# Cross attention with 20 heads: the second batch's output projection in 33 products over 512 tokens, and a written order for every step and transfer

## The chip, the cores and the metric

The kernel runs on one core of one Trainium2 chip. The core has a matrix engine (TensorE, PE in the profile), three engines for elementwise work (VectorE, DVE; ScalarE, ACT; GpSimd, POOL) and a queue that only starts transfers here (SyncE, SP). Data lies in SBUF, 128 partitions wide; TensorE reads SBUF and writes PSUM, eight banks of 128 x 512 numbers of 32 bits, and the other engines bring results back. The metric is the device time of one launch in microseconds (us), the median over several runs. The profile is one execution of the same program, recorded by the hardware; its span runs from the first to the last instruction.

## The reference

Two batches of 2048 tokens with 640 channels attend to 77 text tokens and, separately, to 77 further tokens ("ip"), each of 1024 channels, in 20 heads of 32 channels. All is 32-bit float.

```python
q = split_heads(x @ Wq.T)                       # 2 x 20 x 2048 x 32
k, v = split_heads(text @ Wk.T), split_heads(text @ Wv.T)
k_ip, v_ip = split_heads(ip @ Wk_ip.T), split_heads(ip @ Wv_ip.T)
out = attend(q, k, v) + attend(q, k_ip, v_ip)   # softmax(q k^T / sqrt(32)) v
return merge_heads(out) @ Wo.T + bo + x         # output projection and residual
```

The queries, the output projection and the residual work on 4096 rows of 640; keys and values have only 154 rows per batch.

## The kernel before, in words

All matrices come transposed: channels lie on partitions, in five chunks of 128, and tokens along the free side. A chunk of 128 channels holds four heads. The tokens of a batch are worked on in four blocks of 512 (`TB`), two blocks to a step of 1024 tokens. A step u from 0 to 19 is one chunk and one half of a batch: batch 0 has steps 0 to 9, batch 1 steps 10 to 19; q = u // 2 counts the pairs (chunk, batch) from 0 to 9.

**Names of the steps.** In step u, for three groups s of 384, 384 and 256 tokens: `Rs.u` computes scores on TensorE into four banks (L253), `Ks.u` takes them to SBUF on ScalarE (L265), `Ms.u` finds the row maxima on VectorE (L274), `Ss.u` subtracts them on GpSimd (L279), `Es.u` exponentiates on ScalarE (L285), `Ds.u` sums and inverts on VectorE (L292, L294), `Ns.u` multiplies on GpSimd (L299), and `Ts.u` transposes 32 x 32 blocks in place on VectorE (L306). `q.u.h` computes the queries of half h of step u (L221) and `cq` copies them out on ScalarE (L231). `A.q` multiplies the probabilities of both steps of a chunk with the values (L315) and `CA.q` copies the result to the tile `aT` on ScalarE (L338, L342). `k` and `v` project keys and values (L137), and `SQ` transposes the values in blocks (L148).

**Transfers.** SyncE's queue starts nearly all of them, one after another, in the order in which the program issues them. A block of x is 1280 KB (L207), five blocks' tiles do not fit, so the four tiles `xs` are loaded again and again: batch 1 reads each block once for each of its five chunks, from three of the tiles; the fourth, `xs[XROOM]`, holds sums of weights. The values of a chunk are spread over the tile `v4` in 16 small transfers of 20 KB (L175), two such tiles taking turns. A weight chunk for keys or values is 512 KB (`load_w`, L124), one for queries 320 KB (`load_wq`, L212). Before, these transfers are side effects of other steps: `load_next` issues an x block as soon as the queries that read its tile are issued, followed by the spreads still kept in the list `rest`, `begin` issues weights at the start of a step, and `attend` first issues the spreads left over.

**What sets the order.** `ORDERS` writes down, by hand and for each step, four queues of steps: PE, ACT, DVE and POOL. A loop (ahead of L917) emits from each queue the next step whose forerunners, listed in `need`, have been emitted. Each engine executes its own instructions in the order of emission and waits on semaphores where data of another engine is missing; the order across engines is set by data alone, and that of SyncE's transfers by the emission.

**Output projection.** For each block of 512 tokens the first four channel chunks in and out form a 512 x 512 weight matrix, which is multiplied in seven products of 2 x 2 blocks (a scheme of Strassen's kind) instead of eight. A product reads a sum of token rows (`sum_t`, GpSimd, L414) and a sum of weights (`sum_w`, GpSimd, L384), both of 256 columns per instruction on TensorE (L481); the fifth input chunk is added on top (L491). VectorE adds the banks to the residual tile (`take_product`, L506, L510, L512), which then goes out. The fifth output chunk is an ordinary product (`last_chunk`, L461, and `store_last`, L471). Batch 0's projection is interleaved with the steps of batch 1. For batch 1 all five chunks of attention are complete only after A.9 and CA.9, so its projection is the tail of the kernel:

```python
for m, i in ((1, 0), ("o", 0), ...):            # 28 products and 4 last chunks
    ...
    product(m, 1, i, at[(m, i)])                # 36 Matmults of 256 columns per block i
    take_product(m, 1, i, at[(m, i)])
```

Of the last chunks only the fifth input chunk is left for the tail (`p.0` to `p.3` do the rest before it). The residual of batch 1, all of its x, is loaded for the tail into `acc`, `res`, `pb` and slices of `xs` (L847, L851, L917).

Of the kernel before, what the change touches and what calls it, by code (L numbers as in the profile page):

```python
# [8 lines left out]
F32 = mybir.dt.float32  # L9
# [10 lines left out]
def kernel(  # L20
# [41 lines left out]
    SCALE = 1.0 / float(D) ** 0.5  # L62
    NP = B * NC
# [50 lines left out]
    loaded, used = [], set()  # L114

    def load_w(upto=len(wlist)):

        while len(loaded) < upto:
            n = len(loaded)
            if n >= len(wslots) and n - len(wslots) not in used:  # L120
                return
            src, c = wlist[n]
            w = wslots[n % len(wslots)]
            nc.sync.dma_start(  # L124
                out=w, in_=src[:, ts(c, P)].rearrange("(k p) o -> p k o", p=P)
            )
            loaded.append(w)
# [4 lines left out]
    def project_kv(n, out):  # L132

        load_w()
        t = n % 2
        for k in range(NCC):
            nc.tensor.matmul(  # L137
                keys_in(out), loaded[n][:, k, :], cT[:, k, :, t, :], start=(k == 0), stop=(k == NCC - 1)
            )
        used.add(n)  # L140
# [9 lines left out]
    rest = []  # L150

    def spread_v(q):


        spread_rest(len(rest))
        for g in range(G):
            for r in range(G):
                rest.append((q, g, r))
        spread_rest(G * G // 2 if q == NC - 1 else None)
        if q == NC - 1:  # L160
            rest.extend(["x", "wo"])

    def spread_rest(n=None):
        for _ in range(len(rest) if n is None else min(n, len(rest))):
            w = rest.pop(0)
            if w == "x" and n is None:
                return
            if w == "wo":
                nc.sync.dma_start(out=wo, in_=WoT.rearrange("(c p) o -> p c o", p=P))
                for part in PARTS:  # L170
                    fetch(0, part)
            if w in ("x", "wo"):
                continue
            q, g, r = w
            nc.sync.dma_start(  # L175
                out=v4s[q % 2][r * D : (r + 1) * D, g].rearrange("p k d -> p (k d)"),
                in_=squares(q)[g * D : (g + 1) * D],
            )
# [18 lines left out]
    def load_next(u, h):  # L197

        _, b, c, _ = step_of(u)
        n = place_of(u, h)  # L200
        if b == 0 and (c < NC - 1 or n == XROOM):
            return
        m = late.index((u, h)) + XROOM if b else n
        if m < len(late):
            v, g = late[m]
            tokens = ds(S + (step_of(v)[3] * NH + g) * TB, TB)
            nc.sync.dma_start(out=xs[n], in_=xT[:, tokens].rearrange("(k p) t -> p k t", p=P))  # L207
            spread_rest()
# [20 lines left out]
    def take_queries(u, h, pq):  # L229
        qT = qpool.tile([P, TB], F32, tag="qT", name=f"qT_{u}_{h}")  # L230
        nc.scalar.copy(qT, pq)  # L231
        qTs[(u, h)] = qT
# [38 lines left out]
    def maxima(u, s):  # L271
        n = GROUPS[s][1] * G
        mx = small.tile([P, n, 2], F32, tag=f"mx{n}", name=f"mx_{u}_{s}")
        nc.vector.tensor_reduce(mx, rows_of(u, s), AX.X, ALU.max)  # L274
        maxs[s] = mx

    def subtract(u, s):
        n = GROUPS[s][1] * G
        nc.gpsimd.tensor_tensor(  # L279
            rows_of(u, s), rows_of(u, s), maxs[s].unsqueeze(3).to_broadcast([P, n, 2, L]), ALU.subtract  # L280
        )

    def exponential(u, s):
        e = keys_of(u, s).rearrange("p n g l -> p (n g) l")
        nc.scalar.activation(e, e, AF.Exp, scale=SCALE)  # L285

    rdens = {}

    def sums(u, s):
# [5 lines left out]
        rdens[s] = rden  # L295

    def normalise(u, s):
        n = GROUPS[s][1] * G
        nc.gpsimd.tensor_tensor(  # L299
            rows_of(u, s), rows_of(u, s), rdens[s].unsqueeze(3).to_broadcast([P, n, 2, L]), ALU.mult  # L300
# [225 lines left out]
    for k in (0, half):  # L526
# [4 lines left out]
        load_w(k // half + 1)  # L531
    for _ in range(NH * NC):
        load_x()
    load_w()
# [11 lines left out]
    for t in range(2):  # L546
# [3 lines left out]
        for b in range(B):  # L550
            nc.scalar.copy(kT[:, 0, b, t, :], keys_in(ps)[:, b])

    ORDERS = {
        "0": (
            "1010", "430",
            "R0 R1 R2 F2 F0 F1",
            "K0 K1 K2 E0 E1 E2 C0 C2 C1",
            "M0 C0 M1 M2 D0 D1 D2 T0 C2 C1",
            "S0 S1 S2 N0 N1 N2",
        ),
        "1": (  # L570
            "1000", "26647",
            "F0 R0 R1 F3 F2 R2 F4 F1",
            "C0 K0 K1 K2 C2 E0 C3 C4 E1 E2 C1",
            "SQ M0 M1 T1- C3 C4 M2 T2- D0 D1 C0 D2 T0 C2 C1",
            "S0 S1 S2 N0 N1 N2",
        ),
        "even": (
            "1101", "310",
            "R2 R0 F2 R1 F0 F1 AT",
            "K2 K0 K1 E0 C0 C2 E1 C1 E2 CA",  # L580
            "C0 M0 T1- M1 T2- M2 D0 C2 C1 D1 D2 T0",
            "S0 S1 S2 N0 N1 N2",
        ),
        "odd": (
            "0010", "05244",
            "R0 F3 F0 R2 R1 F4 F2 F1",
            "K0 C3 C0 K2 K1 E0 C2 E2 C4 E1 C1",
            "M0 C4 C1 T1- M2 M1 SQ C2 D0 T2- D2 C0 C3 D1 T0",
            "S0 S2 S1 N0 N2 N1",
        ),  # L590
        "8": (
            "1100", "502",
            "R2 R0 F1 R1 F2 F0 AT",
            "K2 K0 K1 C2 C1 E0 C0 E2 E1 CA",
            "M2 C1 M0 T2- T1- M1 C0 D0 D2 D1 T0 C2",
            "S2 S0 S1 N0 N2 N1",
        ),
        "9": (
            "1101", "020",
            "R0 F0 R2 R1 F2 F1",  # L600
            "C0 K0 K2 K1 E0 E2 C1 C2 E1",
            "SQ M0 T2- C1 C2 M2 M1 D0 T1- C0 D2 D1 T0",
            "S0 S2 S1 N0 N2 N1",
        ),
        "10": (
            "1001", "4110",
# [12 lines left out]
        "12": (
            "0000", "7605",  # L620
            "R1 F0 F2 R0 F1 R2 F3 AT",
            "K1 K0 C0 C1 K2 E0 E1 CA E2",
            "C2 T2- M0 T1- M1 C3 M2 D0 D1 T0 D2",
            "S0 S1 S2 N0 G1 N1 N2",
        ),
        "13": (
            "0011", "560574",
            "F1 R0 F3 R1 R2 F2 F4 F5 F0",
            "K0 C1 K1 K2 E0 E1 E2 C0",
            "C3 M0 M1 M2 C2 T2- D0 D1 C5 D2 C4 T0 T1-",  # L630
# [24 lines left out]
            "0001", "46152",
            "R0 F2 R2 F1 R1 F3 F0 F4",
            "K0 K2 K1 C1 E0 E2 C0 E1",
            "M0 M2 C2 T1- T2- M1 C3 D0 D2 C4 D1 T0",
            "G2 S0 S2 G4 S1 N0 N2 N1",
        ),  # L660
        "18": (
            "0000", "5364",
            "R2 F2 R0 F1 R1 F0 F3 AT",
            "K2 K0 K1 E0 C0 E2 E1 CA",
            "C2 M2 M0 T1- M1 T2- D0 C3 D2 C1 D1 T0",
            "S2 S0 G1 S1 N0 N2 N1",
        ),
        "19": (
            "1110", "033657547",
            "R1 F0 F1 R0 F2 R2 F3 F7 F4 F6 F5 F8",  # L670
            "K1 K0 K2 E1 E0 E2",
            "C0 M1 T2- C1 M0 C2 M2 C3 T1- D0 C4 D1 D2 T0 C5",
            "G3 G2 S1 S0 G4 S2 N0 N1 N2",
        ),
        "20": (
            "0110", "6",
            "F0 AT",
            "CA",
            "T1- T2-",
            "",  # L680
        ),
    }

    OUTPUT = {
        10: "o0 20",
        11: "10 50 30 60",
        12: "70 40",
        13: "o1 21 51 11",  # L690
        14: "31 61",
# [7 lines left out]
    def kind_of(u):  # L699
        if str(u) in ORDERS:  # L700
            return str(u)
# [270 lines left out]
```

## Time and profile before

| what | value |
|---|---|
| time, median of 3 runs | 509.31 us (509.28 to 510.11) |
| span of the profiled execution | 506.7 us |
| granted TensorE clock | 1.000 |
| TensorE busy | 498.3 us, 98% |
| VectorE busy | 391.9 us, 77% |
| ScalarE busy | 242.5 us, 48% |
| GpSimd busy | 395.0 us, 78% |
| moved by transfers | 73.0 MB, mean 144 GB/s |

The page gives for each engine the time in which it executed something, and then the chain of work that ended last: followed back from the last instruction, at each step to what released it. A group of instructions is a line, an engine, an operation and its tiles, with its count, busy time, mean duration and the idle time just before. A 32-bit matmul leaves two records on PE and two weight loads. A table by stretches gives, for each stretch of the span, the length and then busy time and record count of PE, its weight loads, VectorE, ScalarE and GpSimd, then the granted clock, the share of the DMA engines and GB/s.

### The profile page before, as it was taken

What the parts mean: (1) busy time and instruction counts of PE and PEld (TensorE: products, weight loads), DVE (VectorE), ACT (ScalarE), POOL (GpSimd) and SP (SyncE); (2) the same over time, 40 slices, a digit from 0 to 9 for tenths busy, and PEclk for the clock granted to TensorE, in tenths of its full rate; (3) what the DMA queues carried; (4) which work ended last, traced back from release to release, by engine and by line L of the source; (5) the groups of instructions that cost most, each with busy time, mean ns of one, the idle gap of its engine ahead of it and who ended that gap; (6) DMA issues with size and microseconds to landing.
All of it is one profiled execution on the core that took longest, in us unless ns stands there. A gap on an engine that the chain in (4) does not pass through costs nothing.

```text
span 506.7 us, 10153 instructions
## 1 busy us (share of the span) xinstructions
PE 498.3 (98%) x4270; PEld 321.0 (63%) x4270; DVE 391.9 (77%) x347; ACT 242.5 (48%) x423; POOL 395.0 (78%) x163
## 2 busy tenths in 40 slices
PE   9999999999999999999999999999999999999997
PEld 5657557557656565456565656554755775588885
DVE  0079999999899987958997997699899999333333
ACT  1266666666676566645545636454654750100000
POOL 0079999989989988899999997798899999940000
PEclk9999999999999999999999999999999999999999
DMA  8982621331362453885574485168323242641213
GB/s 274 357 210 61 159 69 46 86 92 46 92 185 74 112 198 116 284 314 145 159 237 124 131 260 158 53 178 292 110 72 95 86 162 65 225 147 62 84 41 104
DMA packets 71053, 73.03 MB, mean 144 GB/s; under 512 B 5600, under 2 KB 50912, under 8 KB 71008
## 3 DMA queue, kind: packets, MB, share of 16 engines
q1 hardware_dynamic: 70288, 71.67, 45.9%
q8 instruction: 33, 0.54, 0.5%
q10 hardware_dynamic: 720, 0.72, 0.4%
q14 instruction: 12, 0.10, 0.1%
HBM read 58.61 MB, written 10.49 MB: 136 GB/s over the span
## 4 chain that ended last, share of the span: by engine, by line
PE 86%; DMA 5%; POOL 4%; DVE 1%; SPq 1%; issue 1%; ACT 0%; DVEq 0%; POOLq 0%
PE bank L221 31%; PE bank L481 18%; PE bank L253 9%; PE bank L315 9%; PE bank L137 9%; PE bank L461 5%; PE bank L491 5%; DMA x<-in_x_dram 3%; DMA wo_ct<-in_L_xattn_Wo_dram 2%; POOL pb L299 2%; POOL pb L279 1%; SPq L175 1%; POOL x L384 1%; DMA acc<-in_x_dram 1%; PE bank L541 1%
## 5 line engine op out<-in xcount | busy, mean ns | idle before, releaser
L279 POOL TENSOR_TENSOR pb<-pb,mx 128x1848 f32<-128x1848 f32 (+1 forms) x60 | 175.4, 2941 | 45.3 <-DVE mx L274 45.1
L221 PE MATMUL bank<-x,wq 128*128 128x512 f32 x400 | 180.7, 601 | 0.1
L299 POOL TENSOR_TENSOR pb<-pb,rden 128x1848 f32<-128x1848 f32 (+1 forms) x60 | 175.0, 2939 | 5.2 <-DVE rden L294 5.2
L274 DVE TENSOR_REDUCE mx<-pb 128x24 f32<-128x1848 f32 (+1 forms) x60 | 109.6, 1845 | 33.0 <-ACT pb L265 32.8
L265 ACT COPY pb<-bank 128x462 f32<-128x462 f32 (+1 forms) x240 | 101.7, 535 | 59.3 <-PE bank L253 58.5
L221 PEld LDWEIGHTS bank<-x,wq 128*128 128x128 f32 x400 | 74.1, 191 | 85.0 <-issue 81.7
L292 DVE TENSOR_REDUCE den<-pb 128x24 f32<-128x1848 f32 (+1 forms) x60 | 110.4, 1840 | 17.3 <-ACT pb L285 16.9
L285 ACT ACTIVATE pb<-pb 128x1848 f32<-128x1848 f32 (+1 forms) x60 | 94.9, 1582 | 56.4 <-POOL pb L279 56.2
L306 DVE STREAM_TRANSPOSE pb<-pb 128x1920 f32<-128x1920 f32 (+1 forms) x60 | 114.8, 1923 | 2.1 <-POOL pb L299 2.1
L253 PEld LDWEIGHTS bank<-kT,qT 32*128 32x128 f32 x1280 | 47.4, 184 | 26.3 <-issue 18.0
L253 PE MATMUL bank<-kT,qT 32*128 32x154 f32 x1280 | 58.7, 306 | 0.7 <-ACT vT L899 0.4
L315 PE MATMUL bank<-pb,v 32*32 32x512 f32 x1600 | 55.8, 597 | 1.2 <-ACT pb L265 0.7
L481 PE MATMUL bank<-aT,wo_ct 128*128 128x256 f32 x192 | 47.6, 382 | 1.0 <-DVE acc L512 0.7
L137 PEld LDWEIGHTS bank<-wo_ct,aT 128*128 128x128 f32 x320 | 43.1, 188 | 4.2 <-issue 3.5
L315 PEld LDWEIGHTS bank<-pb,v 32*32 32x32 f32 x1600 | 30.7, 103 | 23.2 <-issue 11.8
L137 PE MATMUL bank<-wo_ct,aT 128*128 128x154 f32 x320 | 45.3, 295 | 0.0
L481 PEld LDWEIGHTS bank<-aT,wo_ct 128*128 128x128 f32 x192 | 36.0, 190 | 11.0 <-issue 3.8
L231 ACT COPY qT<-bank 128x512 f32<-128x512 f32 x40 | 23.1, 588 | 31.4 <-PE bank L221 31.4
L461 PE MATMUL bank<-aT,wo_ct 128*128 128x512 f32 x80 | 36.1, 597 | 0.0
L506 DVE SCALAR_TENSOR_TENSOR pb<-bank,bo_sb,pb 128x256 f32<-128x256 f32 x24 | 10.5, 479 | 26.9 <-PE bank L491 16.4
L491 PE MATMUL bank<-aT,wo_ct 128*128 128x256 f32 x96 | 28.6, 379 | 0.0
L506 DVE SCALAR_TENSOR_TENSOR acc<-bank,bo_sb,acc 128x256 f32<-128x256 f32 x40 | 17.0, 466 | 13.3 <-PE bank L491 6.6
(47 smaller groups left out, 286.2 us busy)
## 6 DMA issues: line engine op xcount, KB each, us to landing
x<-in_x_dram SPq DMA_DIRECT2D x20, 1280.0 KB, 6.9
x<-in_x_dram SPq DMA_DIRECT2D x21, 256.0 KB, 5.2
out_dram<-acc SPq DMA_DIRECT2D x19, 256.0 KB, 2.8
acc<-in_x_dram SPq DMA_DIRECT2D x16, 256.0 KB, 6.7
v<-vS SPq DMA_DIRECT2D x160, 20.0 KB, 1.8
pb<-in_x_dram SPq DMA_DIRECT2D x3, 1024.0 KB, 7.6
wq<-in_L_xattn_Wq_dram SPq DMA_DIRECT2D x9, 320.0 KB, 4.8
aT<-in_L_xattn_Wk_dram SPq DMA_DIRECT2D x5, 512.0 KB, 5.6
```

The lines of the kernel that those rows point to most:

```text
L137: nc.tensor.matmul(keys_in(out), loaded[n][:, k, :], cT[:, k, :, t, :], start=(k == 0), stop=(k == NCC - 1))
L221: nc.tensor.matmul(pq, wqs[q % 3][:, k, :], xs[place_of(u, h)][:, k, :], start=(k == 0), stop=(k == NC - 1),)
L253: nc.tensor.matmul(ps[g][:, ts(t, 2 * L)], qTs[(u, h)][g * D : (g + 1) * D, ts(st, P)], kT[g * D : (g + 1) * D, c, b].rearrange("p t l -> ...
L265: nc.scalar.copy(keys_of(u, s)[:, :, g], ps[g][:, : n * 2 * L].rearrange("p (n l) -> p n l", n=n))
L274: nc.vector.tensor_reduce(mx, rows_of(u, s), AX.X, ALU.max)
L279: nc.gpsimd.tensor_tensor(rows_of(u, s), rows_of(u, s), maxs[s].unsqueeze(3).to_broadcast([P, n, 2, L]), ALU.subtract)
L285: nc.scalar.activation(e, e, AF.Exp, scale=SCALE)
L292: nc.vector.tensor_reduce(den, rows_of(u, s), AX.X, ALU.add)
L299: nc.gpsimd.tensor_tensor(rows_of(u, s), rows_of(u, s), rdens[s].unsqueeze(3).to_broadcast([P, n, 2, L]), ALU.mult)
L306: nc.vector.transpose(p, p)
L315: nc.tensor.matmul(pa[r][g * D : (g + 1) * D, :], v4s[q % 2][rows, g, k, :], zones[rows, :, g, k, :], start=(k == 0), stop=(k == NK - 1),)
L481: nc.tensor.matmul(part, w_of[m][:, kp, op], t_of(m, b, i)[:, kp], start=(op == kp == 0 and m in (1, 2, 5)), stop=(op == 1 and kp == 1 and ...
```

## The change

The hand-written queues and the loop that emitted from them are replaced by one list of words, `SCHEDULE`, emitted from first to last. A word names a step as above (with `@` and the bank or half of PSUM it writes); `G`, `W`, `m`, `cm`, `o`, `co` are batch 0's output projection. Transfers have words of their own: `LX.u.h` an x block, `VS.q.half` eight spreads, `LQ` and `LK` weights, `LO`, `LF`, `LW`, `LA` the output weights and residuals. The scale 1/sqrt(32) is applied where the queries are copied out, no longer in the exponential.

Batch 1's projection is written anew. It now treats its 640 x 512 weight part and the 2048 tokens as a whole: the inputs are split in five chunks of channels, the outputs in four, the tokens in two halves of 1024 columns. 33 products (`F`) take the place of 40: each is one weight block or sum of 128 x 128 (`weight`) times one token sum of 1024 columns (`tokens_of`), in two Matmults of 512 columns. 24 weight sums (`V`) run on VectorE, 25 token sums (`X`) on GpSimd (`.p`) or VectorE (`.d`). Eight chains (`CHAINS`) hold which products are accumulated in a bank in sequence and to which outputs the bank is added after each stage (`Y`, on VectorE); a later product of the chain accumulates on top of the same bank. `DIRECT` is empty, so `exponential_of` and the second form of `maxima` are not used. The sums go to tiles that are free by then: weight sums to the first part of `pb`, token sums to `xs[XROOM]`, to `aT`, to the rest of `pb`, and to rows of `aT` no longer read. The outputs are summed where the residual already lies: three x blocks stay in place after the last queries (`home`), and only the fourth is loaded (`LA`).

```diff
@@ transfers as steps of their own
-    def load_next(u, h):
...
-            nc.sync.dma_start(out=xs[n], in_=xT[:, tokens].rearrange("(k p) t -> p k t", p=P))
-            spread_rest()
+    def spread_v(q, half):
+
+        for g in range(G * half // 2, G * (half + 1) // 2):
+            for r in range(G):
+                nc.sync.dma_start(
+                    out=v4s[q % 2][r * D : (r + 1) * D, g].rearrange("p k d -> p (k d)"),
+                    in_=squares(q)[g * D : (g + 1) * D],
+                )
+
+    def load_block(u, h):
+
+        tokens = ds(S + (step_of(u)[3] * NH + h) * TB, TB)
+        nc.sync.dma_start(
+            out=xs[place_of(u, h)], in_=xT[:, tokens].rearrange("(k p) t -> p k t", p=P)
+        )
@@ the scale
-        nc.scalar.copy(qT, pq)
+        nc.scalar.mul(qT, pq, SCALE)
...
-        nc.scalar.activation(e, e, AF.Exp, scale=SCALE)
+        nc.scalar.activation(e, e, AF.Exp)
@@ the order
-    ORDERS = {
...
-    nc.sync.dma_start(out=last_of(1, XROOM), in_=in_dram_last(xT, 1, XROOM))
-    for i in range(1, NHB):
-        fetch_sums(i)
...
-        product(m, 1, i, at[(m, i)])
-        take_product(m, 1, i, at[(m, i)])
...
+    SCHEDULE = (
...
+        "N1.5 M0.6 R1.6@1 S0.6 T1.5 LQ.6 LK.17 v.3.0@3 LK.16 K1.6 VS.2.1 q.8.0@1 M1.6 E0.6 LQ.5 cv.3.0 T2.5 "
+        "cq.7.1 S1.6 M2.6 A.2@1 LX.10.0 D0.6 LK.15 S2.6 E1.6 cq.8.0 D1.6 N0.6 E2.6 D2.6 CA.2 R0.7@0 k.4.1@4 "
...
+        "VS.8.1 m6.1 G4.1 m2.2@5 E1.14 cm6.1 N0.14 LX.16.1 LX.17.0 cq.16.0 D1.14 LX.18.0 VS.7.0 R0.15@0 N2.14 "
...
+        "cm7.1 S2.15 E0.15 M1.15 D0.15 E2.15 m4.1 S1.15 LX.17.1 co.2 q.17.0@0 D2.15 N0.15 E1.15 cm4.1 cq.16.1 "
...
+        "R2.16@0 q.18.0@6 K2.16 T1.15 S0.16 M2.16 M1.16 E0.16 S2.16 A.7@0 LX.19.1 cq.17.1 D0.16 S1.16 E2.16 "
+        "D2.16 N0.16 CA.7 VS.9.1 m5.2@4 E1.16 N2.16 m1.2@7 LX.18.1 cm5.2 VS.8.0 T0.16 cq.18.0 R0.17@0 m3.2 "
...
+        "p.1@4 M2.19 cm6.3 T1.18 G4.3 E0.19 m7.3 S2.19 D0.19 p.0@5 LW E2.19 cm7.3 N0.19 D1.19 m4.3 D2.19 "
+        "N1.19 p.2@7 T0.19 cm4.3 N2.19 T1.19 LA p.3@6 X.I.p@0 T2.19 A.9@0 V.A X.D.d@1 V.P V.F V.G X.A.d@2 V.Q "
+        "V.E V.T V.C V.L V.H V.U CA.9 V.M V.V V.J F31.0@0 V.D V.N V.X F31.1@1 V.S F0.1@1 X.S.d@3 F0.0@0 "
+        "X.L.p@4 z.2 Y0.0.11 F7.0@3 z.0 V.O yz.2 X.U.p@5 F25.1@2 Y0.1.11 F25.0@7 yz.0 Y6.1.10 z.1 X.K.p@6 "
+        "Y6.0.10 F7.1@5 yz.1 F23.1@1 Y2.1.21 F23.0@0 Y2.1.31 X.Q.p@7 Y2.0.31 z.3 Y0.0.01 F13.1@5 Y0.1.01 "
+        "X.C.p@8 F10.0@4 F24.0@0 Y3.0.21 F20.0@7 V.R F1.1@1 V.I V.B Y2.0.21 X.O.p@9 F20.1@2 yz.3 Y6.0.11 "
+        "F24.1@1 Y6.1.11 F29.0@7 X.T.p@10 F29.1@2 F11.0@4 Y6.1.21 F1.0@0 X.X.p@11 Y6.0.21 Y0.1.00 F10.1@6 "
+        "Y3.0.20 F13.0@3 Y0.0.00 X.G.p@12 F6.1@1 Y3.1.21 F3.0@4 F11.1@6 X.B.d@13 F15.1@5 V.K V.W F30.1@2 "
+        "Y3.0.00 X.E.p@2 F30.0@7 Y3.1.20 Y6.1.20 F21.0@4 F3.1@6 X.M.p@4 Y3.0.01 F8.1@2 Y3.1.00 F4.1@4 Y6.0.20 "
+        "Y6.1.30 X.W.p@5 F21.1@6 F19.1@2 Y3.1.01 F8.0@7 Y2.1.11 X.J.p@3 Y6.1.31 F4.0@6 Y6.0.30 F6.0@0 Y1.0.00 "
+        "F26.1@2 Y1.1.00 X.V.p@7 F15.0@3 Y7.1.21 F19.0@7 F26.0@5 X.N.p@6 Y6.0.31 F2.1@2 Y7.0.21 F22.0@7 "
+        "Y7.1.11 X.P.p@r41 F2.0@5 Y2.0.11 F5.1@2 Y7.0.11 F22.1@3 Y7.1.31 X.H.p@r21 F5.0@5 Y5.1.01 F27.1@2 "
+        "Y5.0.01 Y5.0.31 F18.1@1 X.R.p@r31 Y7.1.30 F16.0@7 Y0.1.10 F18.0@0 Y5.1.31 Y7.0.31 F9.0@7 X.Y.p@9 "
+        "Y0.0.10 F9.1@3 Y7.1.10 F27.0@5 X.F.d@13 F14.0@2 F14.1@0 Y4.0.31 F17.0@6 Y4.1.31 F16.1@3 Y7.0.10 "
+        "Y7.0.30 F12.0@2 Y5.1.21 F17.1@4 Y5.0.21 F12.1@0 Y4.0.00 Y1.1.20 F32.0@2 Y4.1.00 F28.0@2 Y1.1.30 "
+        "Y1.0.30 F32.1@0 Y1.0.20 F28.1@0 Y4.0.20 Y4.1.20 "
+    ).split()
...
+    R_SUMS = (
+        "+01-21 +30+11 +21-31 +31+11 +10-00 +11-10 +30-31 +30+10 +01-00 +01-11 +01-D +21-I +30+C +G+J +D-I "
+        "+M-20 +20-L +E+N +40-41 +11-41 +11-40 +10-40 +C-40 +C-41 +V+20 "
+    ).split()
+    W_SUMS = (
+        "+01+30 -32-13 +10+02 +34-24 +03-01 +01+20 +30+31 +20-E +D-22 +03-A +13-I -32-02+12 +00-10-20 "
+        "-12-10-13 +00+01+02 +14-04-34 -P-11 +H+22+23 +32-J+33 +Q-22-24 -G-01+21-22 +U+03-23 +13-V-33 "
+        "+01-Q-03-21+22+23 "
+    ).split()
+    PRODUCTS = (
+        "04 41, 02 Q, K C, M 00, 30 E, B M, L 20, 34 S, W 30, D X, "
+        "H K, F O, A R, N 21, J N, P T, R D, G F, 11 V, S G, "
+        "Q U, O I, E J, C L, 04 S, T 40, I W, 32 P, U H, X 11, "
+        "V B, 10 A, 22 Y"
+    ).split(", ")
+    CHAINS = (
+        "0,31:+11 23:+01 1,24:+00 6,18:+10",
+        "4:-00 17:-20-30",
+        "7:-21-31 13,15:-11",
+        "10:+21 11:+20 3:+00 21:+01",
+        "14:-31 12:+00 28,32:+20",
+        "22:+01+31 9,16:+21",
+        "25:-10 20:-11 29:-21 30:-20 8:-30 19:-31",
+        "26:-21 2:-11 5:-31 27:-10-30",
+    )
...
+    def place_for(text):
+        if text[0] == "r":
+            return tokens_of(text[1:])
+        n = int(text)
+        if n < 2:
+            flat = xs[XROOM].rearrange("p k t -> p (k t)")[:, ts(n, NH * TB)]
+        elif n < 4:
+            return aT[:, ds(NC * NHB + 2 * (n - 2), NH)]
+        else:
+            flat = pb_flat[:, ds(zone + (n - 4) * NH * TB, NH * TB)]
+        return flat.rearrange("p (i t) -> p i t", t=TB)
+
+    def tokens_of(w):
+        if w.isdigit():
+            return rows_of_attention(1, int(w[0]))[:, ds(NH * int(w[1]), NH)]
+        return places[w]
...
+    def add_part(o, ps, op):
+        t = sum_at(o)
+        if o in untouched:
+            untouched.discard(o)
+            nc.vector.scalar_tensor_tensor(t, t, bo_sb[:, o[0] : o[0] + 1], ps, ALU.add, op)
+        else:
+            nc.vector.tensor_tensor(t, t, ps, op)
+        parts_left[o] -= 1
+        if not parts_left[o]:
+            m, i = o
+            nc.sync.dma_start(out=outT[ts(m, P), ds(S + i * TB, TB)], in_=t)
+    def finish(k, args, where):
+        if k == "LW":
+            for kp in range(2):
+                nc.sync.dma_start(
+                    out=a21[:, kp],
+                    in_=WoT[ts(2 * kp, P), : (NC - 1) * P].rearrange("p (op s o) -> p s op o", s=2, o=P)[:, 1],
+                )
+        elif k == "LA":
+            for u, h in late[-XROOM:]:
+                home[step_of(u)[3] * NH + h] = xs[place_of(u, h)]
+            (fourth,) = set(range(NHB)) - set(home)
+            nc.sync.dma_start(
+                out=acc,
+                in_=xT[: (NC - 1) * P, ds(S + fourth * TB, TB)].rearrange("(o p) t -> p o t", p=P),
+            )
+            nc.sync.dma_start(out=res, in_=xT[ts(NC - 1, P), ds(S + fourth * TB, TB)])
+        elif k == "V":
+            out = weight(args[0])
+            (op, a), *more = terms(W_SUMS[number(args[0])])
+            if not more:
+                nc.vector.tensor_scalar(out, weight(a), -1.0, None, ALU.mult)
+            for n, (o2, b) in enumerate(more):
+                if n == 0 and op == ALU.subtract:
+                    nc.vector.scalar_tensor_tensor(out, weight(a), -1.0, weight(b), ALU.mult, o2)
+                else:
+                    nc.vector.tensor_tensor(out, weight(a) if n == 0 else out, weight(b), o2)
+        elif k == "X":
+            w, e = args
+            (_, a), (op, b) = terms(R_SUMS[number(w)])
+            ra, rb = tokens_of(a), tokens_of(b)
+            places[w] = place_for(where)
+            (nc.vector if e == "d" else nc.gpsimd).tensor_tensor(places[w], ra, rb, op)
+        elif k == "z":
+            i = int(args[0])
+            last_chunk(at[f"p.{i}"], 1, i, (NC - 1,))
+        elif k == "yz":
+            i = int(args[0])
+            add_part((NC - 1, i), at[f"p.{i}"], ALU.add)
+        elif k[0] == "F":
+            m, h = int(k[1:]), int(args[0])
+            c, s = stage_of[m]
+            first = (c, h) not in at
+            if first:
+                at[(c, h)] = banks[int(where)]
+            w, x = PRODUCTS[m].split()
+            nc.tensor.matmul(
+                at[(c, h)], weight(w), tokens_of(x)[:, h], start=first, stop=True, skip_group_check=True
+            )
+        elif k[0] == "Y":
+            c, h, t = int(k[1:]), int(args[0]), args[1]
+            add_part((int(t[0]), NH * int(t[1]) + h), at[(c, h)], sign_of[(c, t)])
+        else:
+            raise ValueError(k)
...
+    for word in SCHEDULE:
+        emit(word)
```

## The prediction

> **What bounds the kernel now.** I read the page's totals first, then its chain, then the table by stretches for the end, then groups, the chain and the DMA queue in order of time.
>
> ```profile
> span 506.7 us, 10153 instructions
> PE 498.3 (98%) x4270; PEld 321.0 (63%) x4270; DVE 391.9 (77%) x347; ACT 242.5 (48%) x423; POOL 395.0 (78%) x163
> ...
> PE 86%; DMA 5%; POOL 4%; DVE 1%; SPq 1%; issue 1%; ACT 0%; DVEq 0%; POOLq 0%
> ```
>
> TensorE works 98% of the span, at granted clock 1.00 in every stretch. So only fewer or shorter matmuls, or new gaps on PE, can move the end. Now the end, us of busy time by engine:
>
> ```profile
> 425.00:437.00 12.00, 11.78 (x175) 5.30 (x173) 5.60 (x5) 0.58 (x3) 11.92 (x9) 1.00 0.42 132
> 437.00:460.00 23.00, 22.89 (x98) 18.67 (x99) 9.36 (x17) 1.72 (x7) 11.70 (x10) 1.00 0.46 160
> 460.00:480.00 20.00, 20.00 (x95) 17.60 (x94) 7.13 (x14) 0.00 (x0) 0.00 (x0) 1.00 0.24 79
> 480.00:507.00 27.00, 22.98 (x107) 19.89 (x105) 8.69 (x17) 0.00 (x0) 0.00 (x0) 1.00 0.23 78
> ```
>
> From 437 PE (first figure after the comma) is full, DVE (third) works 25 us of 66, POOL (fifth) is done by 449. The chain there:
>
> ```profile
> 431.33 5.07 PE bank L315 x137
> 436.39 0.02 issue
> 436.42 0.66 ACT aT L342 x2
> ...
> 437.12 1.99 PE bank L481 x8
> 439.11 3.43 PE bank L461 x8
> ...
> 461.54 7.77 PE bank L481 x36
> ...
> 503.01 0.48 DVE pb L506
> ```
>
> A Matmult leaves two records. 36 records of 256 columns take 7.77 us, so such a Matmult costs 0.432 us; 8 of 512 columns take 3.43, so 0.858. The tail runs from 437.12 to about 503.0 (65.9 us), then 3.7 us to the span's end.
>
> **The change, part by part.** The words after A.9 are the tail; ahead of it the steps on PE, ScalarE, VectorE and GpSimd stand in the same order in both kernels. Only SP's order differs.
>
> *Products.* Gone: 4 blocks x 36 Matmults of 256 columns, 144 x 0.432 = 62.2 us. New: 33 products x 2 halves of 512 columns, 66 x 0.858 = 56.6. The four `z` steps stay, 3.4. PE's tail goes from 65.6 to 60.0: **-5.6 us**.
>
> *Weight sums.* 24 `V` words are 40 VectorE instructions of 128 columns, from SBUF to SBUF, which this trace does not have. Nearest rows:
>
> ```profile
> L512 DVE TENSOR_TENSOR pb<-pb,bank 128x512 f32<-128x512 f32 x9 | 6.2, 687 | 11.2 <-PE bank L481 5.7 <-PE bank L491 5.5
> L506 DVE SCALAR_TENSOR_TENSOR pb<-bank,bo_sb,pb 128x256 f32<-128x256 f32 x24 | 10.5, 479 | 26.9 <-PE bank L491 16.4 <-ACT aT L342 8.6 <-PE bank L481 1.9
> L148 DVE STREAM_TRANSPOSE vS<-vT 128x160 f32<-128x160 f32 x10 | 2.8, 315 | 1.2 <-ACT vT L899 1.2
> L414 POOL TENSOR_TENSOR x<-aT 128x512 f32<-128x512 f32 x10 | 12.6, 1269 | 0.0
> L384 POOL TENSOR_TENSOR x<-wo_ct 128x256 f32<-128x256 f32 x1 | 0.7, 742 | 0.0
> ```
>
> 687 and 479 ns for 512 and 256 columns extrapolate to 0.375 us; the 160-column transpose, busy 2.8/10, gives 0.28. I take 0.29, the row nearest in size. The last transpose ends at 430.6 (427.04 + 3.56). From there 31 of the 40 stand ahead of `X.S`, with the sums `X.D` and `X.A` (1024 columns; the 1280-column transposes take 1.48, so 1.2 each): 31 x 0.29 + 3 x 1.2 = 12.6, so S is ready at 443.2. PE, from 437.12, has F31, F31, F0, F0, z (5 x 0.858) until 441.4; F7 needs S. **+1.8 us** of gap; at 0.375 it is 4.5, and at 0.2 (below any row) none.
>
> *Outputs.* 62 `Y` and 4 `yz` at 0.69 are 45.5 us. With 11.6 for all V and 6.0 for five X.d, VectorE has 63 us between 430.6 and PE's end near 499: it fits, but idle drops from two thirds to a twelfth. `Y` also frees PSUM: a chain's next stage waits for it, and PE is then late. I add 0, bound 2.
>
> *GpSimd.* 256 and 512 columns (742, 1269) extrapolate to 2.33 us for 1024; 20 sums are 47 us. The first runs before A.9 ends; the others start at 436.7 and have until 499. Each of the early ones is ready 4 us or more ahead of its product (L at 439.0 for F23 near 448). Cost 0.
>
> *The port.* What a two-operand VectorE sum costs while GpSimd sums, no row shows: VectorE's sums now have one operand in PSUM, and beside them GpSimd's 1848-column sums keep 3284 ns. Bounds: nothing, or full exclusion (priced as a rival). I take nothing, the rows' own case, and keep the other end. The Trainium skill (SBUF — State Buffer, Who interferes with whom) speaks against it: two SBUF inputs on VectorE contend with a GpSimd instruction that reads SBUF, the later one waiting out the earlier. By it 18 sums alternate with GpSimd's from 436.7 and the result is the second rival's; by the rows it is the sum below.
>
> *Transfers.* Residual loads shrink, as three x blocks stay in place; `LW` (two of 256 KB; such loads land in 3.6 us) goes out after the store at 420.5 and lands near 425, ahead of 430.6. Both are hidden by 5 us or more. The order costs more. Each transfer waits for the eighth before it, and small ones land behind big ones:
>
> ```profile
> 198.24 6.54 DMA x<-in_x_dram
> 204.79 0.51 SPq L175
> ```
>
> An x block lands in 6.3 to 6.5 us, 16 spreads take 16 x 0.63 = 10.1 us of issue. (a) `LX.18.1` now stands behind VS.9.1, whose eight issues start when A.7 (350.8) lets v4 go, about 355.5, so it is issued at 360.4 and lands at 366.7; q.18.1 starts at 365.29 in this trace: **+1.3**. (b) VS.2.1 stands behind LQ.6, LK.17 and LK.16, 1.3 MB issued at 136 that take some 8 us (54.78 to 63.17 in this trace): its last spread lands near 144.5, A.2 is due at 143.55: **+0.9** (0 to 1.6). (c) VS.7.0 stands behind three x blocks, so LX.17.1 goes out at 334 and lands at 340.5 to 342; q.17.1 is due at 341.1, 340.2 without (d): **+0.9** (0 to 2.5). (d) The gap at 331 disappears: there an x block and 16 spreads hold the acc load back to 320.9 and PE waits 0.66 for DVE: **-0.9** with its drain. Sum **+2.2**, bounds -0.9 to +4.5. Gaps near 180 to 191 (3 us) come from ScalarE and stay.
>
> *ScalarE's* scale moves from 60 exponentials to 40 query copies of unchanged shape. 0.
>
> Sum: -5.6 + 1.8 + 2.2 = **-1.6**: span 505.1. The median of the runs shown (509.31) is 2.6 above the profiled span; with that kept, 507.7.
>
> **Rivals.** *VectorE keeps the port while its sums run back to back; GpSimd starts after S.* For it: its queue has no wait among them. Then 19 sums start at 443.2, and V.O, R, I, B, K, W and two X wait up to 2.33 us, which VectorE's spare time half covers: +1 to +4, so 510.
>
> *The engines alternate, one sum each* (the other side). At 436.7 VectorE has done A, D, P, F, G, A and 8 more: 18 of 31 remain. GpSimd has ten sums ready (L to E); the eleventh overwrites L and needs F23, behind F7. So S comes 10 x 2.33 = 23 us later, PE stands idle with it, and the later V and X add 0 to 6: 507.7 + 23 + 0..6, say 533. It decides as soon as three sums wait in turn. Against it: no such wait has a row.
>
> *VectorE becomes the bound.* If V costs 0.375 and Y 0.75 (the 512-column row with bias), its 63 us become 71 from 430.6: last add at 502, no gain, and the transfers' 2.2 remain: 512.
>
> *The change does not do what it says*: 132 records for 288, as the order shows; no chance.
>
> **How the numbers follow.** No contention 0.45 (507.7; own range 504.5 to 511), VectorE first 0.20 (510; 507 to 513), alternation 0.25 (533; 527 to 538), VectorE bound 0.10 (512). 0.2%, 1.0 us, is about what a measurement tells from no change. Faster: 0.6 of the first, 0.35 of the second: 0.35. Same: 0.2, 0.3 and little: 0.16. Slower: 0.49. The range must take half of the alternation: 504.5 leaves out 0.05 below, 533 some 0.13 above.
>
> **What would show it.** Right: L481/L491 gone after A.9, 132 records 0.429 apart, one PE gap of 1 to 3 us four products in, 128-column VectorE sums near 0.29 at any time, GpSimd's near 2.33 from A.9's end; x blocks ending PE's waits before q.17.1 and q.18.1. Wrong: a long VectorE stretch between V.L and X.S with 2.3 us per sum (alternation), GpSimd's second sum starting after X.S (VectorE first), PE gaps ended by DVE all along (VectorE the bound).

## The result and the profile after

| | before | changed |
|---|---|---|
| time, median of 4 runs each | 509.68 us (509.28 to 510.11) | 545.6 us (542.57 to 549.3) |
| ratio, 95% interval | 1 | 1.0715 (1.0666 to 1.0765) |
| span of the profiled execution | 506.7 us | 545.2 us |
| granted clock, mean over the span | 1.000 | 0.969 |
| A.9 starts at | 431.3 us | 444.9 us |
| from there to the span's end | 75.4 us | 100.3 us |

The change makes the kernel 7% slower. The last two rows split the 38.5 us by which the two profiled executions differ (the medians differ by 35.9): 13.6 are lost before the new tail begins, 24.9 in it. The page of the changed kernel (totals, then its chain):

```profile
span 545.2 us, 9882 instructions
PE 503.0 (92%) x4114; PEld 295.7 (54%) x4114; DVE 453.5 (83%) x410; ACT 242.5 (44%) x423; POOL 423.2 (78%) x167
...
PE 74%; DVE 15%; DMA 6%; ACT 2%; issue 1%; SPq 1%; POOL 1%; DVEq 0%
```

TensorE has 156 records fewer and is busy longer, since part of its work ran at a lower clock; it is now idle for 42 us of the span. VectorE, 1% of the chain before, has 15% of it. The same four stretches of the end as in the prediction (busy time of PE, its weight loads, VectorE, ScalarE, GpSimd; then clock, DMA share, GB/s):

```profile
425.00:437.00 12.00, 12.00 (x40) 7.58 (x41) 11.61 (x12) 5.98 (x7) 10.40 (x6) 1.00 0.33 101
437.00:460.00 23.00, 17.96 (x191) 8.25 (x190) 22.72 (x30) 2.31 (x8) 16.86 (x8) 1.00 0.21 69
460.00:480.00 20.00, 3.43 (x4) 1.52 (x5) 18.78 (x17) 0.00 (x0) 14.05 (x6) 0.51 0.03 13
480.00:507.00 27.00, 23.03 (x53) 9.84 (x51) 22.96 (x29) 0.00 (x0) 17.40 (x8) 0.98 0.08 30
```

From 460 to 480 PE does 3.4 us of work at clock 0.51, while VectorE is busy for 18.8 us with 17 instructions, 13 of them sums of 128 columns that take 1.2 us each on average. The timeline of VectorE there (start, duration, instruction); A.9 ends at 450.4:

```profile
443.89 0.71 DVE L812 TENSOR_TENSOR pb<-wo_ct 128x128 f32<-128x128 f32 x1
...
450.44 0.28 DVE L812 TENSOR_TENSOR pb<-wo_ct 128x128 f32<-128x128 f32 x1
450.75 7.03 DVE L812 TENSOR_TENSOR pb<-pb,wo_ct 128x128 f32<-128x128 f32 x3
457.71 2.42 DVE L812 TENSOR_TENSOR pb<-wo_ct,pb 128x128 f32<-128x128 f32 x1
460.05 2.42 DVE L812 TENSOR_TENSOR pb<-wo_ct 128x128 f32<-128x128 f32 x1
462.40 2.42 DVE L810 SCALAR_TENSOR_TENSOR pb<-wo_ct 128x128 f32<-128x128 f32 x1
...
475.30 1.22 DVE L818 TENSOR_TENSOR aT<-aT 128x1024 f32<-128x1024 f32 x1
```

and of GpSimd:

```profile
442.09 2.35 POOL L818 TENSOR_TENSOR x<-aT 128x1024 f32<-128x1024 f32 x1
450.58 2.35 POOL L818 TENSOR_TENSOR pb<-aT,x 128x1024 f32<-128x1024 f32 x1 [6.14 <-DVE pb L812]
452.89 2.39 POOL L818 TENSOR_TENSOR pb<-aT 128x1024 f32<-128x1024 f32 x1
455.25 2.38 POOL L818 TENSOR_TENSOR pb<-aT,x 128x1024 f32<-128x1024 f32 x1
457.60 2.38 POOL L818 TENSOR_TENSOR pb<-aT,pb 128x1024 f32<-128x1024 f32 x1
...
471.67 2.38 POOL L818 TENSOR_TENSOR aT<-aT 128x1024 f32<-128x1024 f32 x1
485.94 2.35 POOL L818 TENSOR_TENSOR pb<-aT,pb 128x1024 f32<-128x1024 f32 x1 [11.89 <-PE bank L832]
```

GpSimd sums follow each other every 2.35 us, and each VectorE sum ends just after a GpSimd sum ends: 457.71 + 2.42 = 460.13, the GpSimd sum begun at 457.60 ended at 459.98. It is one for one. Before 450.58 such VectorE sums took 0.28, all but the first: it met the GpSimd sum begun at 442.09 and lasted 0.71, until just after that one's end at 444.44. The tiles of these two have nothing in common, so it is no dependence in the program that makes the one wait for the other. After ten sums GpSimd stops (its next one overwrites L, which a later product still reads), VectorE's last sums run freely, and the row at 475.30 is X.S, the sum for which F7 waits. The waits of PE from 450 on (what it waited for: us in total, times, longest):

```profile
PE bank L832 <- DVE aT L818: 21.3, 1, 21.3
PE bank L832 <- DVE acc L779: 4.7, 1, 4.7
PE bank L832 <- ACT aT L338: 0.3, 1, 0.3
```

The second is the later cluster (X.B, K, W, at 498 to 507). VectorE's adds out of PSUM are untouched by GpSimd: the groups of the tail in one table show 36 of them at 683 ns (such adds took 687 in the kernel before), with one operand in PSUM, and 20 weight sums, both operands in SBUF, at 1004.

```profile
L779 DVE TENSOR_TENSOR x<-x,bank 128x512 f32<-128x512 f32 x36 | 23.6, 683 | 8.2 <-PE bank L832 7.9
L812 DVE TENSOR_TENSOR pb<-pb,wo_ct 128x128 f32<-128x128 f32 x20 | 19.9, 1004 | 0.6
```

Of the 13.6 us ahead of the tail 0.7 stand at A.2 already, without an account here; the rest lies at three places. The table compares the start of each A with the kernel before:

| | A.2 | A.3 | A.6 | A.7 | A.8 | A.9 |
|---|---|---|---|---|---|---|
| later by, us | 0.7 | 3.0 | 2.9 | 7.1 | 13.6 | 13.6 |

Two of them are waits of PE for an x block, here in PE's timeline (q.17.1 and q.18.1; 10 records otherwise take 4.5, and the granted clock over these two is 0.73 and 0.59):

```profile
346.50 6.23 PE L191 MATMUL bank<-x,wq 128*128 128x512 f32 x10 [3.42 <-DMA x<-in_x_dram]
375.91 7.55 PE L191 MATMUL bank<-x,wq 128*128 128x512 f32 x10 [3.47 <-DMA x<-in_x_dram]
```

And the transfer queue ahead of both (start of the first issue, time to the end of the last one, count):

```profile
322.41 1.63 SPq L176 DMA_DIRECT2D x<-in_x_dram  x3
324.08 13.27 SPq L148 DMA_DIRECT2D v<-vS  x8
...
338.60 0.44 SPq L176 DMA_DIRECT2D x<-in_x_dram  x1
...
362.81 6.18 SPq L148 DMA_DIRECT2D v<-vS  x8
369.04 0.58 SPq L176 DMA_DIRECT2D x<-in_x_dram  x1
```

VS.7.0, eight small spreads behind three x blocks, takes 13.3 us to issue, since the eighth of them goes out at 336.8 only, when the third block has landed; LX.17.1 leaves at 338.6. LX.18.1 leaves at 369.0, behind VS.9.1, which had to wait for A.7.

### The profile page after: what moved, and what is told of

It reads as the page before. It is cut to its first block, busy times and chain, and to the rows that moved or that the text cites. A ratio compares the mean times of both kernels' runs of the same rounds, so it can differ in the third digit from the quotient of the medians.

```text
span 545.2 us, 9882 instructions
## 1 busy us (share of the span) xinstructions
PE 503.0 (92%) x4114; PEld 295.7 (54%) x4114; DVE 453.5 (83%) x410; ACT 242.5 (44%) x423; POOL 423.2 (78%) x167
## 4 chain that ended last, share of the span: by engine, by line
PE 74%; DVE 15%; DMA 6%; ACT 2%; issue 1%; SPq 1%; POOL 1%; DVEq 0%
PE bank L191 29%; PE bank L311 9%; PE bank L832 9%; PE bank L223 9%; PE bank L132 8%; DVE pb L812 6%; PE bank L477 6%; PE bank L457 3%; DMA x<-in_x_dram 3%; DVE den L288 2%; DVE mx L261 2%; DVE pb L302 2%; PE bank L487 2%; DMA aT<-in_L_xattn_Wk_ip_dram 1%; DMA wq<-in_L_xattn_Wq_dram 1%
## 5 line engine op out<-in xcount | busy, mean ns | idle before, releaser
L191 PE MATMUL bank<-x,wq 128*128 128x512 f32 x400 | 185.3, 614 | 7.4 <-DMA x<-in_x_dram 7.2
L191 PEld LDWEIGHTS bank<-x,wq 128*128 128x128 f32 x400 | 75.7, 195 | 95.5 <-issue 82.8
L311 PEld LDWEIGHTS bank<-pb,v 32*32 32x32 f32 x1600 | 31.8, 103 | 21.8 <-issue 10.1
L201 ACT ACTIVATE qT<-bank 128x512 f32<-128x512 f32 x40 | 23.7, 600 | 36.2 <-PE bank L191 36.2
L457 PE MATMUL bank<-aT,wo_ct 128*128 128x512 f32 x80 | 37.4, 609 | 0.0
L832 PE MATMUL bank<-aT,wo_ct 128*128 128x512 f32 x24 | 12.9, 642 | 21.6 <-DVE aT L818 21.3
L477 PE MATMUL bank<-aT,wo_ct 128*128 128x256 f32 x128 | 32.0, 382 | 0.0
L779 DVE TENSOR_TENSOR x<-x,bank 128x512 f32<-128x512 f32 x36 | 23.6, 683 | 8.2 <-PE bank L832 7.9
L477 PEld LDWEIGHTS bank<-aT,wo_ct 128*128 128x128 f32 x128 | 24.0, 190 | 6.7 <-issue 4.0
L457 PEld LDWEIGHTS bank<-aT,wo_ct 128*128 128x128 f32 x80 | 15.2, 193 | 17.8 <-issue 17.5
```

Source lines behind the costliest of these rows:

```text
L191: nc.tensor.matmul(pq, wqs[q % 3][:, k, :], xs[place_of(u, h)][:, k, :], start=(k == 0), stop=(k == NC - 1),)
L311: nc.tensor.matmul(pa[r][g * D : (g + 1) * D, :], v4s[q % 2][rows, g, k, :], zones[rows, :, g, k, :], start=(k == 0), stop=(k == NK - 1),)
L477: nc.tensor.matmul(part, w_of[m][:, kp, op], t_of(m, b, i)[:, kp], start=(op == kp == 0 and m in (1, 2, 5)), stop=(op == 1 and kp == 1 and ...
```

## The experiments

Theory: a VectorE sum of two SBUF operands waits out a GpSimd sum that is running, and the tail loses by that alone; the transfers' order loses the rest, each wait counting twice because the clock falls in it. Rivals: the sums are slow of themselves; the scale, the list or the new tail's loads make the start late; queries after a wait are slow for want of data.

**GpSimd held until X.S.** One small GpSimd instruction that reads X.S stands ahead of X.L:

```diff
             places[w] = place_for(where)
+            if w == "L":
+                s = places["S"][:, 0, :HT]
+                nc.gpsimd.tensor_tensor(places[w][:, 0, :HT], s, s, ALU.add)
```

> The changed kernel, with one GpSimd instruction of 256 columns put ahead of X.L that reads X.S, so that GpSimd's second to twentieth sums cannot start before VectorE has made S; its result is overwritten by X.L and nothing is left out. Theory A (a two-operand VectorE sum from SBUF waits out a GpSimd sum that is running, and the two alternate): the sums between A.9's end and X.S fall from 2.3 us each to 0.2 to 0.3, S is ready about 5 to 6 us after A.9's end instead of 26, PE's wait for it falls from 21.3 us to 0 to 2, and the recovery of its clock goes with it. GpSimd then starts 19 sums of 2.37 us some 5 us later, and later VectorE sums among them still wait: span 522 to 532 against 545.2. Theory B (the sums are long for a reason of VectorE's own, their operands or their place, and GpSimd only happens to run): they stay above 2 us with GpSimd idle, S comes as late as before, GpSimd starts 20 us later and the span goes to 555 to 565.

Span 532.7, A.9 at 444.1, tail 88.6. The sums ahead of X.S run at 0.2 to 0.3 us each, X.S begins 4.1 us after A.9's end (453.66 against 449.6) and PE waits 0.4 us for it in place of 21.3. The rival falls. The span missed the forecast by 0.7 because waits came up further on, here the waits of PE and two rows of VectorE's timeline in this kernel:

```profile
PE bank L833 <- DVE x L777: 6.1, 1, 6.1
PE bank L833 <- DVE acc L777: 5.1, 1, 5.1
PE bank L833 <- DVE x L775: 1.2, 1, 1.2
```
```profile
466.84 5.48 DVE L810 TENSOR_TENSOR pb<-pb,wo_ct 128x128 f32<-128x128 f32 x3
472.24 2.42 DVE L808 SCALAR_TENSOR_TENSOR pb<-wo_ct 128x128 f32<-128x128 f32 x1
```

These are V.R, V.I and V.B, which stand among the outputs and now meet GpSimd's sums; in the changed kernel GpSimd was pausing there. VectorE's queue is in order, so each holds the outputs behind it back, PSUM is not freed, and PE waits.

**The transfers of the kernel before, the new tail.** The words up to A.9 are put in the order in which the old loop emitted steps and transfers; each engine's own steps keep their order (of the diff, the last transfers alone):

```diff
-VS.8.1 ... LX.16.1 LX.17.0 LX.18.0 VS.7.0 LX.17.1 LX.19.0 LX.19.1 VS.9.1 LX.18.1 VS.8.0 VS.9.0
+LX.16.1 LX.17.0 LX.17.1 VS.7.0 VS.7.1 LX.18.0 LX.18.1 LX.19.0 LX.19.1 VS.8.0 VS.8.1 VS.9.0 VS.9.1
...
```

> The changed kernel with the transfers up to A.9 issued in the order of the kernel before (x blocks, spreads, weights); each engine's steps and the whole tail unchanged. Theory A (the 13.6 us by which A.9 starts later come from SP's order alone: an x block behind spreads, and the clock that drops in each wait): A.9 starts at 431 to 432 as in the kernel before, the tail stays near 100 us, span 530 to 533. Theory B (the scale on the query copies, or the list's emission, holds the steps up): A.9 still starts after 440, span 542 to 547.

Span 531.8; A.9 at 431.5, the tail 100.3 as in the changed kernel. The scale on the query copies and the list cost nothing to speak of: the transfers' order is 13.4 of the 13.6 us.

**The new transfers, the tail of the kernel before.**

```diff
-F31.0@0 ... Y4.1.20
+product(m, 1, i, at[(m, i)]) ...      # the old tail and its residual loads
```

The other words of the new tail, its loads `LW` and `LA` among them, go too; the old residual loads stand in step 19.

> The other half of the change alone: the list with its own transfers up to A.9, then the tail of the kernel before (28 products of seven per block, four last chunks, its residual loads). If the two parts add up: A.9 starts at 444 to 446, the tail takes the 75.4 us of before, span 519 to 522. If the new residuals or the new tail caused part of the late transfers: A.9 below 441, span below 517.

Span 517.0, A.9 at 441.6, tail 75.4. A.9 lies between the two forecasts, so the start of A.9 alone does not decide. The issue times do: the changed kernel's new loads go out from 431.7 on, when A.8 (409.4) has long started with its 13.6 us of delay; here A.8 is 10.3 late, and the old loads follow it, from 410.6 on. So the tail's loads are not what makes the start late. The parts nearly add up: 10.3 here, 25.1 in the run before it, 35.4 of the 38.5 seen at once; the rest is within what the spans of the changed kernel differ by (540.8 to 547.5 in four runs). In this run q.18.1 waited 3.06 us and took 6.09, for 3.47 and 7.55. With the new order of transfers as it stands A.9 came 10.3, 12.8 and 13.6 us late in three traces (this run, GpSimd held, the changed kernel).

**Both edits together.** The order of the second kernel and the GpSimd instruction of the first.

> Both edits together: transfers of the kernel before, new tail, GpSimd's sums held until X.S. If both causes are separate, the gains add: 545.2 - 13.6 - (14 to 23) = 508.6 to 518 for the span. Under theory A of the port the VectorE sums after X.S that meet GpSimd's still cost, so it stays above the 506.7 of before; if the port mattered only ahead of X.S, it falls below, to 502 to 505.

Span 520.2, A.9 at 431.8, tail 88.4: the first edit's tail and the second's start. It ends above the 508.6 to 518 of the first line, for the reason the first experiment showed: PE waits of 6.1, 5.6 and 1.2 us behind V.R to V.B, X.B to V.W, and V.O. So the conflict is not one at the head of the tail; it is there wherever a VectorE sum stands while GpSimd sums.

**All of VectorE's sums first.** From the last kernel: the six remaining weight sums and X.L go right behind X.S on VectorE, GpSimd is held until V.W, and the four z products cover the time.

```diff
-V.S F0.1@1 X.S.d@3 F0.0@0 X.L.p@4 z.2 Y0.0.11 F7.0@3 z.0 V.O ...
+V.S F0.1@1 X.S.d@3 V.O V.R V.I V.B V.K V.W X.L.d@4 F0.0@0 z.2 z.0 z.3 z.1 Y0.0.11 F7.0@3 ...
-            if w == "L":
-                s = places["S"][:, 0, :HT]
+            if w == "U":
+                s = weight("W")
...
```

> New tail with the transfers of the kernel before, and VectorE's sums gathered: the last six weight sums (V.O, R, I, B, K, W) follow X.S at once, X.L moves to VectorE behind them, and a GpSimd instruction of 128 columns that reads W holds GpSimd's remaining 18 sums until then; the four z products go ahead of F7. Nothing is left out. Theory A (all of the tail's loss is two-operand VectorE sums waiting out GpSimd's): 40 weight sums of 0.25 and four token sums of 1.2 us from 430.6 end near 446, no 128-column sum takes over 0.7 us, PE's waits come to 3 to 4 us, none long enough for the clock to fall, and the tail takes 75.4 - 5.6 + 3 to 4 = 73 to 74 us: span 504 to 506 against 506.7, ratio 0.994 to 0.999. Rival: GpSimd, which starts 14 us after A.9's start and has 18 sums of 2.37 us, becomes the bound (PE waits for GpSimd), span 508 to 512, ratio over 1.002.

Faster than both kernels, than the kernel before by 0.5%, which is small but clear of the noise: 506.28 us (505.34 to 507.25, 6 runs) against 508.87 of the kernel before (11 runs), ratio 0.9947 (0.9933 to 0.9962). The page, then a group and PE's waits in its tail:

```profile
span 504.5 us, 9894 instructions
PE 494.0 (98%) x4114; PEld 290.9 (58%) x4114; DVE 427.1 (85%) x411; ACT 242.7 (48%) x423; POOL 421.5 (84%) x167
```
```profile
L810 DVE TENSOR_TENSOR pb<-pb,wo_ct 128x128 f32<-128x128 f32 x20 | 5.5, 290 | 0.6
```
```profile
PE bank L833 <- DVE x L775: 1.2, 2, 0.8
PE bank L833 <- ACT aT L338: 0.3, 1, 0.3
PE bank L833 <- DVE res L775: 0.2, 1, 0.2
```

The same 20 sums take 290 ns for 1004. PE waits 1.7 us in the whole tail, never for GpSimd, and the tail takes 72.1 us for 75.4. A.9 starts 1.1 us later than in the kernel before; that remainder was not looked into. The gathered sums, the later start of GpSimd and the z products moved ahead came in one step; what each is worth alone was not run.

**One x block moved.** Step (a) of the prediction alone:

```diff
-VS.9.1 m5.2@4 E1.16 N2.16 m1.2@7 LX.18.1
+LX.18.1 VS.9.1 m5.2@4 E1.16 N2.16 m1.2@7
```

> The changed kernel with one word moved: LX.18.1 ahead of VS.9.1. Step (a) of the prediction alone. If the eight spreads that wait for A.7 hold the block, it is issued near 358 and lands by 366, q.18.1's wait of 3.47 us goes and with it the slow Matmults after it (7.55 us for 4.45): A.9 starts 6 to 7 us earlier than 444.9, at 438 to 439, and the tail keeps its 100 us. If the block was late for the DMA engines' load, the wait stays within 1 us of 3.5.

Span 540.4, A.9 at 438.7: the wait and the slow queries after it are gone, 6.1 us as forecast. The wait ahead of q.17.1 stays (3.36).

**Three places undone.** In addition VS.7.0 behind LX.17.1 and VS.2.1 ahead of LQ.6:

```diff
-LQ.6 LK.17 v.3.0@3 LK.16 K1.6 VS.2.1 ... LX.18.0 VS.7.0 ... LX.17.1
+VS.2.1 LQ.6 LK.17 v.3.0@3 LK.16 K1.6 ... LX.18.0 ... LX.17.1 VS.7.0
```

> The changed kernel with the three places of the prediction's steps (a), (b), (c) undone: LX.18.1 ahead of VS.9.1, VS.7.0 behind LX.17.1, VS.2.1 ahead of LQ.6, LK.17 and LK.16. If these three carry the 13.6 us: A.9 starts at 431 to 433, no wait of PE for an x block over 0.5 us. If other places matter too (x blocks that now go two or three at a time): A.9 stays at 434 or later, with waits that move to other blocks.

Span 533.0, A.9 at 432.7, no wait for an x block above 0.5 us. In PE's timeline:

```profile
143.77 5.52 PE L311 MATMUL bank<-pb,v 32*32 32x512 f32 x160
...
151.48 0.80 PE L223 MATMUL bank<-kT,qT 32*128 32x154 f32 x13 [1.47 <-issue]
...
342.51 4.56 PE L191 MATMUL bank<-x,wq 128*128 128x512 f32 x10
...
366.72 4.56 PE L191 MATMUL bank<-x,wq 128*128 128x512 f32 x10
```

q.17.1 and q.18.1 start at once. A.2 takes 5.52 us again (6.41 in the changed kernel, which held its end back behind VS.2.1), but a wait of 1.47 in the scores after it, put on nothing, keeps A.3 2.3 us late; by A.7 1.4 of it is left, which is what A.9 has too.

**The same, with 1.8 MB behind k.4.1.**

```diff
-A.2@1 LX.10.0 D0.6 LK.15 S2.6 ... k.4.1@4
+A.2@1 D0.6 S2.6 ... k.4.1@4 LK.15 LX.10.0
```

> The kernel of e7 with LX.10.0 and LK.15 issued behind k.4.1 (some 6 us later) in place of at A.2. Undoing step (b) took the wait inside A.2 away (5.52 us again) and left a wait of 1.47 us in the scores after it, which the profile puts on nothing (issue), so that A.3 stayed 2.3 us late. Theory A (these waits come from the 1.8 MB in flight just then): none over 0.3 us between 144 and 155, A.3 starts at 180.9 to 181.6. Theory B (they lie at a place in PE's instruction stream whatever is in flight): a wait of 1 to 1.5 us stays near 150 and A.3 starts at 182.5 to 183.5.

Span 533.0; the wait near 150 is 0.81 us, A.3 starts at 182.4. This tells nothing: LX.10.0 still went out at 144.1 (143.9 in the run before) and LK.15 even earlier than there, at 139.8 for 144.3, since SyncE runs ahead of the words of other engines and only its own order and the tile's readers bind it. What makes these waits of about 1 us stays open.

**Work in place of the wait.** Four Matmults whose result is overwritten, where PE would wait:

```diff
             at[name] = banks[int(where)]
+            if name in ("q.17.1", "q.18.1"):
+                keys = kT.rearrange("p c b t l -> p (c b t l)")
+                for _ in range(4):
+                    nc.tensor.matmul(at[name], keys[:, :P], keys[:, TB : 2 * TB], start=True, stop=True)
```

> The changed kernel with four Matmults of 512 columns on the keys' tile, their result overwritten, put ahead of q.17.1 and of q.18.1, so that PE works (4 x 0.858 = 3.4 us) where it had waited 3.4 us. Theory A (each wait costs twice, since the granted clock falls after some 3 us of idle PE): the x blocks land when they did, but q.17.1 takes 4.5 us in place of 6.2 and q.18.1 4.5 in place of 7.5; A.9 starts 3 to 5 us earlier than 444.9. Theory B (the queries after a wait are slow because their block is still landing or for want of weights): they stay slow, and A.9 starts at 444 to 448.

```profile
348.19 4.46 PE L191 MATMUL bank<-x,wq 128*128 128x512 f32 x10
...
375.82 4.45 PE L191 MATMUL bank<-x,wq 128*128 128x512 f32 x10
```

Span 542.0, A.9 at 441.7. The queries take 4.46 and 4.45 us for 6.23 and 7.55, at granted clock 1.00 for 0.73 and 0.59, and q.18.1 starts at 375.8 as before: the block came no earlier, only the clock was kept. The two groups are 4.9 us shorter; A.9 gains 3.2, since A.3 came 1.8 us later in this run. So a wait of 3.4 us cost 1.8 to 3.1 more behind it, and work that does nothing saves that. Why A.3 came later is in this run's timeline:

```profile
152.19 0.80 PE L223 MATMUL bank<-kT,qT 32*128 32x154 f32 x13 [1.12 <-issue]
152.92 6.14 PE L132 MATMUL bank<-wo_ct,aT 128*128 128x154 f32 x32
```

These 32 records take 4.48 in the changed kernel; here the clock is 0.72 from 153 to 159. A wait of only 1.12 us stands ahead of them, where waits of 1.35 and 1.47 at the same place (GpSimd held, three places undone) were followed by 4.48. So the length of a wait does not settle alone whether the clock falls. Nor does it take 3.4 us: with GpSimd held, with the old tail and with one block moved, waits of 3.02 to 3.36 us ahead of q.17.1 or q.18.1 were followed by queries of 5.93 to 6.23 us at clock 0.73 to 0.76. The shortest, with GpSimd held:

```profile
376.62 6.05 PE L191 MATMUL bank<-x,wq 128*128 128x512 f32 x10 [3.02 <-DMA x<-in_x_dram]
```

## Why the prediction was wrong, step by step

The forecast was 507.7 with 0.35 for faster; the measured 545.6 lies beyond the range's 533. Two steps failed, the port, which the sum put at nothing, and the transfers, which it put at 2.2; a third price, the clock, had no term. The second rival's 533, with transfers at 13.6 in place of 2.2, gives 544.4. That this comes so near is partly luck: the rival has no term for the clock either, worth 3.6 us in the tail, and the 13.6 are those of the one profiled execution.

- *The port* ("I take nothing, the rows' own case") is the step that failed first. The mechanism was there as the second rival, with 0.25: GpSimd starting at A.9's end, ten sums, then a stop at L, S 23 us late, PE idle with it. Measured 21.3, and 4.7 for the later sums where it gave 0 to 6. What was wrong was the evidence: GpSimd's unchanged 3284 ns beside VectorE's reductions, transposes and PSUM adds says nothing of sums with both operands in SBUF, which none of those rows has. The runs show that these meet: 0.2 to 0.3 us alone, 2.3 to 2.4 beside GpSimd, 683 ns with a PSUM operand in either case. The Trainium skill (SBUF — State Buffer, Who interferes with whom) had said just this, two SBUF inputs contend and the later waits, and all runs here agree; by it the forecast would have been the second rival's. The runs show that such sums wait for each other, not through what.
- *Transfers*, +2.2 with bounds -0.9 to 4.5, measured 13.6. (a) 1.3 was 6.1 (the experiment that moves LX.18.1 alone; 6.5 in the table): a wait of 3.47, since VS.9.1 took 6.2 us to issue for the 4.9 of the forecast and the block 6.9 to arrive for 6.3, and 3.0 for the slow queries after it. That A.7 came 7.1 late changed nothing in this, as it moved the block and q.18.1 alike. (c) and (d), 0.9 and -0.9, were 4.2 together, from A.6 to A.7. The gap at 331 went, as (d) said; but LX.17.1, which was to leave at 334 and land at 340.5 to 342, left at 338.6, and PE had it at 346.5: 335.7 and 343.6 without the 2.9 us by which A.6 was late. That is a wait of 3.42, and the slow queries add 1.7. (b) 0.9 was 2.3: 0.9 inside A.2 as forecast, and a wait after it that no run explained. The gaps near 180 to 191, read as 3 us from ScalarE, are 0.52 put on nothing and 0.38 on ScalarE in the trace; the sum does not use them.
- *A price that had no term*: the clock. The profile before has no PE gap over 1.1 us and clock 1.00 throughout, so each gap was priced at its length. The filled waits show the surcharge, 4.9 us for two, and in the tail PE is busy 64.7 us for 61.2 at full clock in the version with the sums first: another 3.6. The Trainium skill (TensorE: Matmul & The Clock Gate, The HAM clock gate) puts the drop to half after an idle window of about 3.4 us. The waits of 3.42 and 3.47 us fit that; others do not. In other runs waits of 3.02 to 3.36 us ahead of the same two groups were followed by slow queries too, and one wait of 1.12 us by clock 0.72, while others of 0.8 to 1.5 cost nothing more. So here 3.0 us were enough each time, between 1.5 and 3.0 us no wait was seen in these places, and below that it went either way.
- *Products*, -5.6: right in kind, -4.7 in size (61.2 us of PE busy for 65.9 from A.9's end).
- *Weight sums*: 0.29 each, 0.26 alone (13.9 us less three token sums of 1.2, over 40, in the version with the sums first). The wait for S of 1.8, free of GpSimd, was 0.4 to 0.7.
- *Outputs and GpSimd*, 0: right. The adds took 683 and 744 ns, PE waited 1.4 us for them in the version with the sums first, within the bound of 2, and in no tail shown here did PE wait for GpSimd. *ScalarE's scale*, 0: right. *VectorE as the bound* did not come up: in the version with the sums first it is idle for 12 us of the tail's 67.

## What to carry to other kernels

Before giving VectorE sums of two SBUF tensors beside GpSimd sums, ask for each pair whether they can run at the same moment: the order of words on different queues does not keep them apart, only a dependence does. Short sums suffer most, since each one waits for a whole long one; gathered ahead of GpSimd's run, they cost their own time. On a queue of transfers, a small one behind big ones takes their time (13.3 us for eight spreads behind three blocks), and a block that was late for TensorE by 3.0 to 3.5 us cost another 1.4 to 3 us by the clock.

## What the runs showed of the hardware

GpSimd hardly notices the short sums that it delays: 2.38 us beside them, 2.35 alone. Against a VectorE sum of 1024 columns it waits too: its sum at 498.9 took 3.34 us, and the 128-column instruction of the version with the sums first 1.22, where one of 256 columns took 0.61 with GpSimd held until X.S. The spread between executions was 1.2% in the changed kernel (542.57 to 549.3, four runs), with its waits and its falling clock, against 0.2% (509.28 to 510.11, four runs) to 0.4% (508.09 to 509.91, eleven runs) in the kernel before and 0.4% in the version with the sums first. That the clock makes this difference is likely, not shown.
